# Local attention layers: norm products and half of a key projection placed between the halves of the products with values

## The chip, the cores and the metric

The kernel runs on one core of a Trainium2 chip. A core has five engines with instruction streams of their own: TensorE (PE; its weight loads are shown as PEld), VectorE (DVE), ScalarE (ACT), GpSimd (POOL) and SyncE (SP, which here issues the DMAs). They meet at semaphores. TensorE reads SBUF and writes PSUM. The metric is the device time of one execution in microseconds, and the median of several runs is compared.

## The reference

The program is two transformer blocks over an input of 4 sequences x 512 tokens x 128 features, float32. The first has causal attention with 16 heads and a mixture of experts, the second causal attention with 4 heads and, as its second half, a small network of six layers with local attention. The change touches only those six layers. Cut to what matters, one of them is:

```python
qkv = shift_tokens(x) @ Wqkv                 # 16 heads of 64
q = l2norm(q) * qs ;  k = l2norm(k) * ksc    # divided by the norm over the 64 features
q, k = rotary(q), rotary(k)
# windows of 32 tokens: each query window sees the window before it and its own
sim = einsum('bhwie,bhwje->bhwij', bq, bk2) * 8.0    # 32 x 64 for each window
attn = softmax(where(mask, -big, sim))
out = einsum('bhwij,bhwje->bhwie', attn, bv2)
x = out @ Wo + x
x = ffn(shift_tokens(x)) + x                 # layer norm, gated GELU, 128 -> 2 x 341 -> 128
```

## The kernel before, in words

The local layers hold the features on the partitions and 512 tokens of one sequence in the free dimension. The work is cut into *cells*: one cell is one layer, one sequence and a group of 4 heads, so there are 6 x 4 x 4 = 96. Four cells in a row share a sequence; after the fourth comes the feed-forward part of that sequence, `feed`, a generator cut in pieces that `place("N")`, `place("L")`, ..., `place("D")` put between the steps of later cells, one piece at a place of the right name.

The order of the instructions on each engine is the order in which the program emits them (`tc.manual_schedule()`); no planner moves anything. The loop over `n` works on several cells at once: it computes scores and attention of cell `n`, the last products with values of cell `n-1`, the norms and values of cell `n+2`, and the projections of cell `nx = n+3`. These are the steps that matter here, with their lines in the profile of before:

- `project(n, w)` (L831): queries (`w = 0`) or keys (`w = 1`), two products 128 x 128 by 128 x 512, the halves `h = 0, 1` of one PSUM tile `pq` of which there is a single buffer.
- `rotate` (L842, L843 on DVE, L844, L845 on POOL) reads `pq` into `qr` or `kr`; `square` (L850 on ACT) reads it too, into `sq`, and with that `pq` is free.
- `norms` (L860): eight products with 32 output rows each sum the squares into a PSUM tile `nb`; then DVE's maximum (L869), Ln and Exp on ACT with a table load each (L871, L873), and four DMAs by SP that spread the factors into `rb` (L879). `scale` (L887 on POOL) multiplies `kr` and `qr` by them.
- `values` (L898): four products into two PSUM tiles, copied by ACT (L905) and shifted by three DMAs.
- `scores(n, u)`, `u = 0, 1` (L921 masks, L928): 64 small products of 32 x 32 by 32 x 64, then DVE's maximum and subtraction (L937, L939). `exponential` (L948), `normalise` (L953 to L955), `turn` (L962 transposes on TensorE, L964 copy `pT` by ACT).
- `weigh(n, u)` (L977): 32 small products of 64 x 64 by 64 x 32 of `pT` with the values, into two PSUM tiles `po2` and `po2b`, copied out by ACT (L989). `po2b` shares its buffer with the transposes.
- `output` (L997) and `feed` (L1010 hidden products `phf`, L1015 gelu, L1025, L1033, L1061).

Each of these float32 products stands in the trace as two matmul records with two weight loads. The PSUM tiles `nb`, the values' two, the output's and all of feed's come from one pool of two buffers (`bank`).

TensorE's order in one turn of the loop is: `scores(n, 0)`, `weigh(n-1, 1)`, `norms(n+2)`, sometimes a piece of feed, `project(nx, 0)`, in every other cell `output`, `scores(n, 1)`, `values(n+2)`, sometimes a piece of feed, `turn(n, 0)`, `project(nx, 1)`, `weigh(n, 0)`, a piece of feed, `turn(n, 1)`. ScalarE's is: copies of `weigh(n-1, 1)`, `exponential(n, 0)`, Ln and Exp of the norms, `square(nx, 0)`, copies of values, `exponential(n, 1)`, `pT` of `turn(n, 0)`, copies of `weigh(n, 0)`, `pT` of `turn(n, 1)`, `square(nx, 1)`, and after that a piece of feed (in two cells of four one or two gelus with a table load).

Of the kernel before, what the change touches and what calls it, by code (L numbers as in the profile page):

```python
# [17 lines left out]
F32 = mybir.dt.float32  # L18
BF16 = mybir.dt.bfloat16
AF = mybir.ActivationFunctionType  # L20
ALU = mybir.AluOpType
# [3 lines left out]
B, S, D = 4, 512, 128  # L25
P = 128
# [20 lines left out]
def adaln_kernel(ctx: ExitStack, tc: tile.TileContext, a: dict):  # L47
# [4 lines left out]
    vec, pool_e = nc.vector, nc.gpsimd  # L52
# [192 lines left out]
    chain, rush, dense, norms = [], [], [], []  # L245
# [268 lines left out]
    def project(b):  # L514
        hT = zT[b]
        qk = io.tile([P, 2, 4, S], F32, name="qk0", bufs=3)
        v = io.tile([P, TB, H0 + 3, HD0 + 1], F32, name="v0")
        proj[b] = qk, v.rearrange("p t h d -> p t (h d)")
        for j in range(4):
            pp = ps_s.tile([P, 2, S], F32, name="pp", tag="s")  # L520
            for w in range(2):
                mm(pp[:, w, :], wqk[:, w, j, :], hT, start=True, stop=True)
            if j % 2 == 0:
                vec.tensor_scalar(
                    qk[:, 0, j, :], pp[:, 0, :], sb[:, 0, 1 + j : 2 + j], sb[:, 0, 0:1], ALU.add, ALU.mult
                )
                vec.tensor_scalar(qk[:, 1, j, :], pp[:, 1, :], sb[:, 1, 1 + j : 2 + j], None, ALU.add)
            else:
                act(qk[:, 0, j, :], pp[:, 0, :], AF.Identity, bias=sbq[:, j : j + 1], scale=sb[:, 0, 0:1])
                act(qk[:, 1, j, :], pp[:, 1, :], AF.Identity, bias=sb[:, 1, 1 + j : 2 + j])  # L530

            if j in (0, 3):
                js = slice(0, 1) if j == 0 else slice(1, 4)
                for w, row in ((0, HD0 + 1), (1, HD0)):
                    nc.sync.dma_start(qk[row::32, w, js, :], a["pos0"][w, :, js, :])
            if j in (0, 3):
                done.update(("project", b, x) for x in range(j + 1))
            yield
        pv = ps.tile([P, S], F32, name="pv0", tag="small")
        for t in range(TB):  # L540
            mm(pv[:, t * P : (t + 1) * P], hT[:, t * P : (t + 1) * P], wv, start=True, stop=True)


        pool_e.memset(v[:, :, H0:, :], 0.0)
        pool_e.memset(v[:, :, 0:H0, HD0 : HD0 + 1], 1.0)
        for t in range(TB):
            vec.tensor_tensor(
                v[:, t, 0:H0, 0:HD0],
                pv[:, t * P : (t + 1) * P].rearrange("p (h d) -> p h d", h=H0),
                bv.rearrange("p (h d) -> p h d", h=H0),  # L550
                ALU.add,
            )
        done.add(("values", b))
        yield
# [171 lines left out]
    while todo or late or ripe or pend:  # L726
        admit()
        if todo and (todo[0][1] or todo[0][0].start()):
            u, s = todo.pop(0)
# [37 lines left out]
    with ExitStack() as ph:  # L767
# [13 lines left out]
        def bank(name, shape=(P, S)):  # L781
            return ps_g.tile(list(shape), F32, name=name, tag="g")
# [9 lines left out]
        NC = len(cells)  # L792
# [29 lines left out]
            pool_e.tensor_scalar(t, t, g, None, ALU.mult)  # L822


        def project(n, w):
            l, b, j = cells[n]
            d = live.setdefault(n, {})
            pq = d["pq"] = ps_q.tile([P, 2, S], F32, name="pq")
            for h in range(2):
                c0 = w * INNER + (2 * j + h) * P  # L830
                mm(pq[:, h, :], layers[l][0][:, c0 : c0 + P], shifted[b], start=True, stop=True)  # L831

# [18 lines left out]

        def norms(n):

            d = live[n]
            nb = bank("nb", (P, S // 2))
            for h in range(2):
                for w in range(2):
                    for x in range(2):
                        c = 32 * (2 * w + x)
                        mm(  # L860
                            nb[c : c + 32, :],
                            nsel,
                            d["sq", w][:, h, x * (S // 2) : (x + 1) * (S // 2)],
                            start=(h == 0),
                            stop=(h == 1),
                            skip_group_check=True,
                        )
            rn = att.tile([P, S // 2], F32, name="rn")
            vec.tensor_scalar(rn, nb, 1e-24, None, ALU.max)  # L869
            place("N")  # L870
            act(rn, rn, AF.Ln, scale=65536.0)  # L871
            place("L")
            act(rn, rn, AF.Exp, scale=-0.5, bias=nsh_t)  # L873
            place("X")
            rb = d["rb"] = work.tile([P, 2, S], F32, name="rb", bufs=1)
            for w in range(2):
                for x in range(2):
                    c = 32 * (2 * w + x)
                    nc.sync.dma_start(  # L879
                        rb[:, w, x * (S // 2) : (x + 1) * (S // 2)],  # L880
                        rn[c : c + 32, :].unsqueeze(1).broadcast_to([32, 4, S // 2]),
                    )
# [80 lines left out]
            pT = live[n]["pT", u] = att.tile([P, 4, P], F32, name="pT2")  # L963
            nc.scalar.copy(pT, pt)  # L964

        def weigh(n, u):
            d = live[n]
            pT = d.pop(("pT", u))

            po = [ps_o.tile([P, 2, 4, WIN], F32, name="po2"), ps_t.tile([P, 2, 4, WIN], F32, name="po2b", tag="pt2")]  # L970
            for i in range(4):
                for x in range(4):
                    c = 64 * (x % 2)
                    for w in range(2):
                        r = slice(64 * w, 64 * w + 64)
                        c1 = 32 * ((x + w) % 4)
                        mm(  # L977
                            po[w][c : c + 64, x // 2, i, :],
                            d["v"][(w + i) % 2][r, 2 * u + i // 2, 64 * x : 64 * x + 64],
                            pT[r, i, c1 : c1 + 32],  # L980
                            start=True,
                            stop=True,
                        )
            if u == 0:
                d["o"] = cel.tile([P, 2, 2, S // 2], F32, name="oT2", bufs=3)
            o = d["o"][:, u].rearrange("p h (a w q) -> p (h a) w q", w=4, q=WIN)
            for w in range(2):
                y = po[w].rearrange("p h (a b) q -> p (h a) b q", b=2)
                nc.scalar.copy(o[:, :, 0::3, :] if w else o[:, :, 1:3, :], y)  # L989
# [93 lines left out]
        for n in range(-4, NC + 1):  # L1083
            nx = n + 3 if 0 <= n + 3 < NC else None
            here = 0 <= n < NC
            if here:
                scores(n, 0)
            if 0 <= n + 1 < NC:
                scale(n + 1)
            if n > 0:  # L1090
                weigh(n - 1, 1)
            if here:
                exponential(n, 0)
            if 0 <= n + 2 < NC:
                norms(n + 2)
            elif n + 2 >= NC:
                for name in "NLX":
                    place(name)
            place("C")
            if nx is not None:  # L1100
                l, b, j = cells[nx]
                if l + 1 < DEPTH:
                    if (b, j) == (2, 0):
                        layers[l + 1] = load_layer(l + 1)
                    if (b, j) == (2, 1):
                        load_rotations(l + 1)
                project(nx, 0)
            if here:
                normalise(n, 0)
            if nx is not None:  # L1110
                rotate(nx, 0)
            if n > 0 and cells[n - 1][2] % 2 == 1:
                output(n - 1)
            place("Z")
            if n + 4 < NC and cells[n + 4][2] == 0:
                b = cells[n + 4][1]
                shifted[b] = shift_in(b, xss[b % 2])
            if here:
                scores(n, 1)
            if nx is not None:  # L1120
                square(nx, 0)
            if 0 <= n + 2 < NC:
                values(n + 2)
            if here:
                exponential(n, 1)
            place("A")
            if here:
                turn(n, 0)
                normalise(n, 1)
            if nx is not None:  # L1130
                project(nx, 1)
                rotate(nx, 1)
            if here:
                weigh(n, 0)
            place("B")
            if here:
                turn(n, 1)
            if nx is not None:
                square(nx, 1)
                l, b, j = cells[nx]  # L1140
                for b1, j1, w, h in turns:
                    if (b1, j1) == (b, j) and l + 1 < DEPTH:
                        rotations(l + 1, w, h)
            place("D")
# [107 lines left out]
```

## Time and profile before

| | |
|---|---|
| three runs | 2582.3, 2593.25, 2601.71 us; median 2593.25 us |
| the profiled execution | 2575.9 us, span 2574.1 us, mean granted TensorE clock 0.955 |
| local layers | from 647 to 2569 us of the span, 96 cells |
| PE busy / weight loads | 2292.4 us (89%) / 1365.4 us (53%), 45916 instructions each |
| DVE, ACT, POOL busy | 1511.2 us (59%), 1402.9 us (55%), 1068.7 us (42%) |
| the chain that ended last | PE 73%, issue 9%, DVE 8%, ACT 8% |
| DMA queues | q1: data, 21.8% of 16 engines; q8: instructions, 359 packets, 5.88 MB |

How to read it: a row of the groups names line, engine, operation, tiles written and read, shapes and count, then the busy time and the mean length of one in ns, then the time the engine stood idle just before these instructions and what ended it. "issue" there means that nothing in the profile was waited for. The rows of the timeline begin with the start in us and the length. The matmuls overlap, so the distance between the starts of two records tells what one costs, not its length.

### The profile page before, as it was taken

What the parts mean: (1) busy time and instruction counts of PE and PEld (TensorE: products, weight loads), DVE (VectorE), ACT (ScalarE), POOL (GpSimd) and SP (SyncE); (2) the same over time, 40 slices, a digit from 0 to 9 for tenths busy, and PEclk for the clock granted to TensorE, in tenths of its full rate; (3) what the DMA queues carried; (4) which work ended last, traced back from release to release, by engine and by line L of the source; (5) the groups of instructions that cost most, each with busy time, mean ns of one, the idle gap of its engine ahead of it and who ended that gap; (6) DMA issues with size and microseconds to landing.
All of it is one profiled execution on the core that took longest, in us unless ns stands there. A gap on an engine that the chain in (4) does not pass through costs nothing.

```text
span 2574.1 us, 99974 instructions
## 1 busy us (share of the span) xinstructions
PE 2292.4 (89%) x45916; PEld 1365.4 (53%) x45916; DVE 1511.2 (59%) x2258; ACT 1402.9 (55%) x2211; POOL 1068.7 (42%) x692
## 2 busy tenths in 40 slices
PE   7899999877689999989999899998999899999997
PEld 3345454442355555556555555555555555556553
DVE  3354544343466666666666676665666667666763
ACT  1233336433456666566566566665665656666653
POOL 1000100110644664446545465544754546545540
PEclk9899999898888999989999999999999999999998
DMA  2100000000224222242222432234222333232220
GB/s 71 62 3 1 2 2 1 1 1 25 66 55 131 71 59 66 66 124 59 65 68 58 124 74 59 64 90 111 51 69 64 99 91 73 52 74 59 63 74 14
DMA packets 103408, 152.01 MB, mean 59 GB/s; under 512 B 16454, under 2 KB 78092, under 8 KB 101964
## 3 DMA queue, kind: packets, MB, share of 16 engines
q1 hardware_dynamic: 102988, 145.63, 21.8%
q8 instruction: 359, 5.88, 1.0%
q14 instruction: 61, 0.50, 0.1%
HBM read 34.27 MB, written 1.05 MB: 14 GB/s over the span
## 4 chain that ended last, share of the span: by engine, by line
PE 73%; issue 9%; DVE 8%; ACT 8%; DMA 1%; SPq 1%; POOL 1%; ACTq 0%; DVEq 0%; POOLq 0%
PE pq L831 12%; PE s L928 8%; PE py L997 6%; PE po L977 6%; PE phf L1010 5%; PE pv L898 5%; PE s L286 4%; PE nb L860 4%; PE pt L962 3%; PE pyf L1061 3%; PE ye L360 2%; PE po2b L977 2%; PE p L342 2%; DVE ur L843 1%; DVE qr L842 1%
## 5 line engine op out<-in xcount | busy, mean ns | idle before, releaser
L831 PE MATMUL pq<-xs,wqkv 128*128 128x512 f32 x768 | 395.5, 640 | 13.6 <-ACT sq L850 11.8
L844 POOL TENSOR_TENSOR kr<-kr,ur 128x512 f32<-128x512 f32 x96 | 122.1, 1272 | 540.1 <-DVE ur L843 512.6
L928 PE MATMUL s<-kr,qr 32*32 32x64 f32 x24576 | 296.9, 224 | 25.8 <-issue 25.6
L928 PEld LDWEIGHTS s<-kr,qr 32*32 32x32 f32 x24576 | 260.0, 103 | 71.8 <-issue 70.5
L850 ACT ACTIVATE sq<-pq 128x1024 f32<-128x1024 f32 x192 | 197.1, 1027 | 127.0 <-DVE ur L843 115.8
L937 DVE TENSOR_REDUCE nm<-s 128x8 f32<-128x512 f32 x192 | 132.2, 689 | 207.6 <-PE s L928 207.4
L844 POOL TENSOR_TENSOR qr<-qr,ur 128x512 f32<-128x512 f32 x96 | 122.8, 1279 | 309.4 <-DVE ur L843 276.1
L831 PEld LDWEIGHTS pq<-xs,wqkv 128*128 128x128 f32 x768 | 142.2, 204 | 172.9 <-issue 153.4
L887 POOL TENSOR_TENSOR qr<-qr,rb 128x1024 f32<-128x1024 f32 x96 | 233.3, 2430 | 0.0
L843 DVE TENSOR_TENSOR ur<-pq,tabs 128x1024 f32<-128x1024 f32 x192 | 232.9, 1213 | 0.0
L887 POOL TENSOR_TENSOR kr<-kr,rb 128x1024 f32<-128x1024 f32 x96 | 228.0, 2375 | 8.2 <-DMA rb<-rn 8.2
L989 ACT COPY oT<-po 128x256 f32<-128x256 f32 x192 | 71.4, 372 | 287.1 <-PE po2b L977 263.8
L964 ACT COPY pT<-pt 128x512 f32<-128x512 f32 x192 | 112.7, 587 | 193.5 <-PE pt L962 193.5
L404 ACT ACTIVATE p<-s 128x1024 f32<-128x1024 f32 (+3 forms) x160 | 104.0, 701 | 189.0 <-PE s L286 148.9
L173 POOL TENSOR_TENSOR ln_rs<-ln_rs,mhalf 128x4 f32<-128x4 f32 x16 | 16.8, 1049 | 436.9 <-DVE ln_rs L172 436.9
L953 DVE TENSOR_REDUCE sm<-p 128x8 f32<-128x512 f32 x192 | 130.6, 680 | 110.7 <-ACT p L948 110.5
L898 PE MATMUL pv<-wqkv,xs 128*128 128x256 f32 x768 | 191.2, 392 | 0.7 <-DVE qr L842 0.7
L977 PE MATMUL po<-pT,vo 64*64 64x32 f32 x3072 | 168.2, 224 | 19.7 <-issue 13.2
L977 PE MATMUL po2b<-pT,vo 64*64 64x32 f32 x3072 | 166.8, 222 | 19.3 <-issue 19.3
L977 PE MATMUL po<-pT,ve 64*64 64x32 f32 x3072 | 166.7, 222 | 19.0 <-issue 19.0
L977 PEld LDWEIGHTS po<-pT,vo 64*64 64x64 f32 x3072 | 129.1, 136 | 96.3 <-ACT pT L964 61.8
L977 PE MATMUL po2b<-pT,ve 64*64 64x32 f32 x3072 | 167.5, 224 | 11.0 <-issue 10.9
(198 smaller groups left out, 4954.6 us busy)
## 6 DMA issues: line engine op xcount, KB each, us to landing
rb<-rn SPq DMA_DIRECT2D x384, 128.0 KB
ve<-vo SPq DMA_DIRECT2D x96, 256.0 KB
tabs<-in_rope_dram SPq DMA_DIRECT2D x12, 1024.0 KB
ve<-vo SPq DMA_DIRECT2D x96, 128.0 KB
wqkv<-in_Wqkv_dram SPq DMA_DIRECT2D x6, 1536.0 KB
ve<-vo SPq DMA_DIRECT2D x96, 96.0 KB
wo<-in_Wo_dram SPq DMA_DIRECT2D x6, 512.0 KB
xs<-zT SPq DMA_DIRECT2D x24, 128.0 KB
```

Of the source, the lines that this page charges most:

```text
L831: mm(pq[:, h, :], layers[l][0][:, c0 : c0 + P], shifted[b], start=True, stop=True)
L843: vec.tensor_tensor(u, d["pq"], t[:, 2 * w + 1], ALU.mult)
L844: pool_e.tensor_tensor(r[:, 0, :], r[:, 0, :], u[:, 1, :], ALU.subtract)
L850: act(d["sq", w], d.pop("pq"), AF.Square)
L887: pool_e.tensor_tensor(t, t, d["rb"][:, w, :].unsqueeze(1).broadcast_to([P, 2, S]), ALU.mult)
L898: mm(pv[:, t, :], shifted[b][:, (y + t) * P : (y + t + 1) * P], layers[l][0][:, c0 : c0 + 4 * HDW], start=True, stop=True,)
L928: mm(s[c : c + 32, w, i, :], q[r, h, t0 : t0 + WIN], k[r, h, t0 : t0 + GK], start=False, stop=(h == 1), skip_group_check=True,)
L937: vec.reduce_max(nm, s, axis=AX.X)
L953: vec.reduce_sum(sm, p, axis=AX.X)
L977: mm(po[w][c : c + 64, x // 2, i, :], d["v"][(w + i) % 2][r, 2 * u + i // 2, 64 * x : 64 * x + 64], pT[r, i, c1 : c1 + 32], start=True, st ...
L997: mm(py, layers[l][1][:, 2 * j - 2 + y, :], o[:, :, y % 2, :], start=(y == 0), stop=(y == 3))
L1010: mm(t[0:m], w1[:, w * DI + r0 : w * DI + r0 + m], xn, start=True, stop=True)
```

## The change

`norms` is cut in two: the products stay in `norms`, and the maximum, Ln, Exp and DMAs become `factors`, at the place where all stood before. `weigh` gets a function to call between its second and third index `i`, that is after 16 of its 32 products. For `weigh(n-1, 1)` this function is `norms(n+2)`; for `weigh(n, 0)` it is the second half (`h = 1`) of `project(nx, 1)`, whose first half stands ahead of `weigh(n, 0)`. `rotate(nx, 1)` is now emitted after `weigh(n, 0)`; on the engines that it uses, DVE and POOL, nothing of weigh stands, so the order there is the same. The orders of ACT, DVE, POOL and SP are as before; TensorE's is not. Computation, tiles and buffers are the same.

```diff
-        def project(n, w):
+        def project(n, w, halves=(0, 1)):
             l, b, j = cells[n]
             d = live.setdefault(n, {})
-            pq = d["pq"] = ps_q.tile([P, 2, S], F32, name="pq")
-            for h in range(2):
+            if 0 in halves:
+                d["pq"] = ps_q.tile([P, 2, S], F32, name="pq")
+            pq = d["pq"]
+            for h in halves:
                 c0 = w * INNER + (2 * j + h) * P
...
         def norms(n):
 
+            if not 0 <= n < NC:
+                return
             d = live[n]
-            nb = bank("nb", (P, S // 2))
+            nb = d["nb"] = bank("nb", (P, S // 2))
...
+
+        def factors(n):
+
+            d = live[n]
             rn = att.tile([P, S // 2], F32, name="rn")
-            vec.tensor_scalar(rn, nb, 1e-24, None, ALU.max)
+            vec.tensor_scalar(rn, d.pop("nb"), 1e-24, None, ALU.max)
...
-        def weigh(n, u):
+        def weigh(n, u, middle):
...
             for i in range(4):
+                if i == 2:
+                    middle()
                 for x in range(4):
...
             if n > 0:
-                weigh(n - 1, 1)
+                weigh(n - 1, 1, lambda: norms(n + 2))
+            else:
+                norms(n + 2)
             if here:
                 exponential(n, 0)
             if 0 <= n + 2 < NC:
-                norms(n + 2)
+                factors(n + 2)
...
+            def half(h):
+                if nx is not None:
+                    project(nx, 1, (h,))
+
+            half(0)
+            if here:
+                weigh(n, 0, lambda: half(1))
+            else:
+                half(1)
             if nx is not None:
-                project(nx, 1)
                 rotate(nx, 1)
-            if here:
-                weigh(n, 0)
```

## The prediction

> **What bounds the kernel now.** I read the page first, then TensorE's timeline in the local layers, then the list of waits, then a table of short stretches for the clock.
>
> The page says who is busy and how many instructions TensorE has to be fed:
>
> ```profile
> PE 2292.4 (89%) x45916; PEld 1365.4 (53%) x45916; DVE 1511.2 (59%) x2258; ACT 1402.9 (55%) x2211; POOL 1068.7 (42%) x692
> ...
> q8 instruction: 359, 5.88, 1.0%
> ...
> L928 PE MATMUL s<-kr,qr 32*32 32x64 f32 x24576 | 296.9, 224 | 25.8 <-issue 25.6
> ...
> L977 PE MATMUL po<-pT,vo 64*64 64x32 f32 x3072 | 168.2, 224 | 19.7 <-issue 13.2
> ```
>
> TensorE is busy 89% of the span; in the local layers (647 to 2569 us, 96 cells, 20.0 us each) one block follows on the other. So every TensorE moment there counts, and an edit on another engine counts only where TensorE waits for it. Second, 45916 matmuls and as many weight loads came in 359 instruction packets: 91832 / 359 = 256 instructions a packet. Third, both small-tile groups lose idle time to "issue", which is no other engine. The timeline shows what that is, here in the middle of one weigh block:
>
> ```profile
> 1508.79 0.22 PE L977 MATMUL po<-pT,ve 64*64 64x32 f32 x1
> 1510.31 0.19 PE L977 MATMUL po2b<-pT,vo 64*64 64x32 f32 x1 [1.31 <-issue]
> ```
>
> Counted over the matmul records, 41 gaps above 0.25 us stand inside weigh blocks (71.7 us) and 28 inside scores blocks (31.8 us), practically all at a record whose number leaves 193 or 194 on division by 256. Work resumes about 2.3 to 2.7 us after an instruction packet started, and packets that follow each other fastest start 3.3 to 3.5 us apart. So I read: 256 instructions that run in less than about 3.4 us make TensorE wait for the next 256. A scores block is 256 instructions in 1.41 us and a weigh block 128 in 0.93, and `scores(n, 0)` and `weigh(n-1, 1)` stand back to back. What such a gap can cost on top is in the table of stretches (busy times, then granted clock, DMA share, GB/s):
>
> ```profile
> 1034.30:1037.70 3.40, 1.66 (x125) 1.46 (x108) 1.38 (x2) 3.37 (x5) 3.40 (x3) 1.00 0.03 7
> 1037.70:1041.10 3.40, 3.31 (x19) 1.39 (x19) 1.11 (x2) 3.06 (x5) 3.34 (x2) 0.50 0.02 5
> ```
>
> After a stretch with TensorE half idle the next 3.4 us run at half clock. Between 646 and 2560 us the half clock holds for 126 us, some 63 us of work lost.
>
> **The part that saves.** At the first join the eight norm products stand between the halves of weigh. If the boundary falls into the second half (64 instructions a cell, so 96 x 64 / 256 = 24 boundaries), the last 256 instructions now took 0.70 (128 of scores) + 0.13 (leaving scores) + 0.23 (half of the second weigh half) + 0.60 (first half and its exit) + 1.1 (norms) = 2.75 us where they took 0.88 + 0.13 + 0.70 = 1.7. The wait falls from 1.7 to 0.65: 24 x 1.05 = **-26 us**. A boundary in scores, in the first half or in the norms themselves (2.2 us there after, 2.3 before) waits as long as now. At the second join there is nothing to save: `weigh(n, 0)` follows values, transposes and a projection, over 4 us with few instructions.
>
> **More changes of tile shape.** The sum needs what it costs TensorE to go from one tile shape to another. Three pairs of rows of its timeline, each the last record of a block and the first of the next:
>
> ```profile
> 1512.88 1.02 PE L831 MATMUL pq<-xs,wqkv 128*128 128x512 f32 x2
> 1513.73 0.59 PE L997 MATMUL py<-oT,wo 128*128 128x512 f32 x1
> ...
> 1522.44 0.59 PE L831 MATMUL pq<-xs,wqkv 128*128 128x512 f32 x1
> 1522.96 0.24 PE L977 MATMUL po<-pT,vo 64*64 64x32 f32 x1
> ...
> 1523.88 0.22 PE L977 MATMUL po2b<-pT,vo 64*64 64x32 f32 x1
> 1524.03 1.09 PE L1010 MATMUL phf<-l_xc,w 128*85 128x512 f32 x2
> ```
>
> Same shape: two pq records take 0.85 to py, 0.43 each. From pq to weigh: 0.52, so 0.09 for the change. From weigh: 0.15 to the next shape, where weigh's own records follow at 0.0147, so 0.135. The first pq after another shape takes 0.53 to the second, 0.10 more. First join: weigh is left once more, 0.135. Second join: pq left once more 0.09, weigh left once more 0.135, pq entered once more 0.10: 0.33. Together 0.46 a cell, x 96 = **+44 us**. The step from norms into weigh is in no row of the trace; norms into pq takes 0.31 against 0.21 for four norms records and I take the same. Ends 30 and 60. This is also where a rule speaks against the change: the Trainium skill, TensorEngine Tiling, Key Properties, says that changing the tiling mode (not the tile) drains TensorE. It gives no figure; a full drain by the records' lengths would be 0.22 - 0.015 at each of two exits from weigh and 0.59 - 0.43 at one from pq, 0.57 a cell, 55 us. The rows say 44, and I take them.
>
> **Less cover for the transposes' copy.** `weigh(n, 0)` needs pT, which ScalarE copies last of its row of work:
>
> ```profile
> 1521.40 0.64 ACT L948 ACTIVATE p<-p 128x512 f32<-128x512 f32 x1
> 1521.93 0.58 ACT L964 COPY pT<-pt 128x512 f32<-128x512 f32 x1
> ```
>
> pT stands at 1522.51, weigh starts at 1522.96: 0.45 spare, because a whole key projection lies in front. With half of it (2 records of 0.43) weigh is reached 0.86 earlier. In four cells in a row the spare time is 0.05, 0.45, 1.03, 0.46 (weigh at 1503.30, 1522.96, 1542.24, 1563.13), and 0.05 of it is the semaphore. New waits: 0.86, 0.46, 0, 0.45; mean 0.44, x 96 = **+42 us**. Nothing wins that back: the other half of the projection comes later in full. Ends 30 and 55. Behind the waiting weigh stand the second half of pq and all else on TensorE; rotate, which needs both halves, was 0.1 to 1.8 us late for other reasons and slips by about as much as TensorE.
>
> **The norms come earlier, the weigh copies later.** The list of waits has both places:
>
> ```profile
> PE phf L1010 <- ACT vo L905: 29.3, 22, 1.8
> ...
> PE nb L860 <- ACT ge L1015: 16.2, 20, 1.0
> ```
>
> The norms' PSUM bank is one that a gelu frees, in two cells of four. Norms are reached 0.46 earlier, so the 20 waits grow by that, 9 us, and the 28 such cells without a wait by a little: **+12** (0 to 22). Half of weigh is now queued behind the wait. Its copies by ScalarE, and the exponential behind them, come later by the norms and the change of shape, 1.1 us, in every cell. In most this is lost in slack: the copies of values wait 0.3 to 1.5 us for TensorE in the plain cells, or normalise's multiply waits out GpSimd's product with the scales anyway (started at 1571.61 it took 2.31 us, and 0.69 where GpSimd is idle). It isn't in the cell with the third gelu: there weigh ended at 1529.20 and the copies ran at 1529.85; now the norms wait until 1530.0, weigh ends near 1531.7, the table load that began at 1530.49 begins near 1532.4, 1.9 later. Exponential, normalise, rotate, square, the copies of values follow in line, and phf waits for those. TensorE itself is 0.6 later, so the 1.4 us wait grows by 1.3 (0 to 1.7): 22 x 1.3 = **+29 us**. The norms' own way (maximum, Ln, Exp, four DMAs by SP) still comes behind that exponential, and its result is needed a cell later.
>
> **Half clock.** Of the gaps between 1.5 and 2.1 us 7 in 36 were followed by half clock, of those above 2.1 us 7 in 12; the cost is 1.7 us or more each. 24 gaps shrink (5 fewer episodes), 22 grow to near 2.7 us (up to 12 more): **+10**, between -15 and +25. The Trainium skill, TensorE: Matmul & The Clock Gate, asks for no idle gap over about 3 us. By that neither kind of gap would count and the term would be 0; the rows above show half clock after 1.8 us, so I keep it.
>
> **Sum.** -26 + 44 + 42 + 12 + 29 + 10 = +111 us. The profiled execution took 2575.9 us (span 2574.1, 1.8 around it), giving 2687; the median of the runs shown is 2593.25, giving 2704. I say **2695**, between the two.
>
> **Rivals.** (1) *Faster by better fetching.* If the spacing took away all of weigh's issue gaps (72 us) and half of the half-clock loss (30), and pT proved hidden, -102 + 44 = -58: about 2520 to 2535. It decides only from 86 us of gain on, the shape changes plus pT, more than all weigh gaps together. For it: the gaps stand where the norms go. Against: scores are left whole, so boundaries in the first half of weigh and in the norms (96 of 160 instructions) wait as before, and those in the second half still 0.65. (2) *No change*: changing shape is hidden under the pT wait and the 1.3 us of phf don't come: 42 - 26 - 10 = +6, about 2590. Against: the shape rows are the same in every cell. (3) *Much slower*: the 1.1 us later exponential goes through to pT in every cell, since ScalarE's work is one line: 96 x 1.1 = 106 more, about 2800. Against: the slack in the plain cells. (4) *Milder*: half of the costs, +40 to +60, about 2640.
>
> **Numbers.** Forecast 0.66, milder 0.10, much slower 0.10, no change 0.08, faster 0.06. The unknown costs span about +55 to +175; the range 2625 to 2765 leaves out (1), (2) and most of (3). A measurement of this kernel can tell about 1% from no change: slower 0.86, same 0.08, faster 0.06.
>
> **What would show it.** Right: waits of weigh for pT grow from some 60 to over 100 us; phf's for the copies of values from 29 to near 60; norms' for gelu grow; issue gaps in weigh fall from 72 to about 45, in scores they stay; a TensorE step of 0.15 stands between weigh and norms twice a cell. Wrong: pT waits unchanged, or issue gaps down by more than 60, or the half clock down by more than half.

## The result, and the profile after

The changed kernel takes 2713.52 us (median of 4 runs, 2708.16 to 2716.03) against 2587.78 us of the kernel before: ratio 1.0479, 95% interval 1.0424 to 1.0534, 126 us slower. The forecast was 2695 in a range of 2625 to 2765. The profiled execution took 2716.03 us with a span of 2714.1.

From the page of the changed kernel, the rows that answer to those shown of before, and one that was small before:

```profile
PE 2366.7 (87%) x45916; PEld 1386.5 (51%) x45916; DVE 1510.0 (56%) x2258; ACT 1401.2 (52%) x2211; POOL 1064.4 (39%) x692
...
L936 PE MATMUL s<-kr,qr 32*32 32x64 f32 x24576 | 290.6, 224 | 9.9 <-issue 9.6
...
L1022 PE MATMUL phf<-l_xc,w 128*128 128x512 f32 (+1 forms) x288 | 170.3, 722 | 63.5 <-ACT vo L913 59.5
...
L989 PE MATMUL po<-pT,vo 64*64 64x32 f32 x3072 | 176.6, 227 | 54.1 <-ACT pT L972 45.1
```

The same 45916 matmuls, but TensorE is shown busy 74 us longer (the granted clock is 0.945 after 0.955) and idle 66 us longer. In the last row pT has taken the place of "issue" as the main reason for idle time ahead of weigh, and the idle time ahead of scores has fallen from 25.8 to 9.9 us, which the prediction did not have. The list of waits has the three places that grew, and the two that shrank:

```profile
PE phf L1022 <- ACT vo L913: 59.5, 22, 3.3
...
PE po L989 <- ACT pT L972: 45.1, 75, 2.6
...
PE nb L864 <- ACT ge L1027: 40.9, 34, 1.4
...
PE po L989 <- issue: 26.7, 18, 5.0
...
PE s L936 <- issue: 9.6, 10, 1.9
```

Before, phf waited 29.3 us and the norms 16.2, in the rows shown ahead; the other three were

```profile
PE po L977 <- issue: 32.2, 19, 4.3
...
PE s L928 <- issue: 25.6, 26, 3.3
...
PE po L977 <- ACT pT L964: 6.3, 4, 2.1
```

Each row gives the total in us, how many times, and the longest.

For the balance I use the local layers alone, from the first projection's record to TensorE's last, since no edit touches what stands ahead of them and that part varies with the clock (647 to 668 us in the profiles). "Busy" is TensorE's busy time there and "half" the time at half clock, busy or not. "Gaps" are the issue gaps over 0.25 us inside blocks of weigh and scores, from the start of one record to the start of the next. The last four columns are waits. All are in us, each row from one profiled execution, which lies up to 17 us from its kernel's median (before: 12 under it), so a few us between two rows carry no weight.

| kernel | local | busy | half | gaps weigh | gaps scores | weigh for pT | norms for gelu | phf for values | pq for square |
|---|---|---|---|---|---|---|---|---|---|
| before | 1922 | 1742 | 138 | 72 | 32 | 6 | 16 | 29 | 12 |
| changed | 2056 | 1810 | 186 | 52 | 13 | 45 | 41 | 60 | 16 |
| second join only | 1977 | 1773 | 124 | 72 | 14 | 42 | 18 | 32 | 10 |
| first join only | 1984 | 1761 | 155 | 52 | 34 | 6 | 38 | 59 | 13 |
| product again, inside | 2019 | 1845 | 124 | 81 | 10 | 5 | 20 | 33 | 10 |
| product again, ahead | 1999 | 1814 | 121 | 85 | 11 | 5 | 18 | 37 | 13 |
| changed, exponential first | 1943 | 1760 | 80 | 52 | 10 | 41 | 40 | 14 | 8 |
| changed, turn first | 1987 | 1779 | 124 | 46 | 14 | 12 | 45 | 50 | 20 |
| before, exponential first | 1905 | 1736 | 121 | 72 | 25 | 5 | 16 | 23 | 13 |
| queries between | 1913 | 1750 | 145 | 16 | 34 | 5 | 0 | 63 | 36 |
| changed, both moves | 1889 | 1749 | 66 | 39 | 18 | 9 | 43 | 6 | 9 |
| before, both moves | 1915 | 1742 | 148 | 83 | 25 | 2 | 19 | 18 | 12 |
| before, exponential and values first | 1867 | 1721 | 93 | 74 | 22 | 5 | 17 | 0 | 12 |
| queries between, values first | 1841 | 1722 | 73 | 15 | 38 | 5 | 0 | 9 | 42 |

The expectations below use an earlier count of the half clock that left out stretches at both ends of the local layers (113 us before, 174 changed, 133 with the queries between).

The changed kernel's 134 us in the local layers are then 66 us of idle time (local less busy: 181 to 247 us) and 68 us of busy time. The idle time is phf +30, pT +39, gelu +25, square +4, issue -32 (as gaps from start to start -39: weigh -20, scores -19). Of the busy time some 24 us are half clock, if half of the 48 us more at half speed is lost. The other 44 us no wait explains, and the steps between tile shapes were put at 44. These steps stand in the trace. At full clock and without a wait, the changed kernel takes in the median 0.149 us from weigh to pq (150 times), 0.522 from pq to weigh (102), 0.309 from norms to weigh (85) and 0.533 from the first pq record after weigh to the next (149), where pq after the transposes takes 0.432.

### The profile page after: what moved, and what is told of

It reads as the page before. It is cut to its first block, busy times and chain, and to the rows that moved or that the text cites. A ratio compares the mean times of both kernels' runs of the same rounds, so it can differ in the third digit from the quotient of the medians.

```text
span 2714.1 us, 99997 instructions
## 1 busy us (share of the span) xinstructions
PE 2366.7 (87%) x45916; PEld 1386.5 (51%) x45916; DVE 1510.0 (56%) x2258; ACT 1401.2 (52%) x2211; POOL 1064.4 (39%) x692
## 3 DMA queue, kind: packets, MB, share of 16 engines
HBM read 34.27 MB, written 1.05 MB: 13 GB/s over the span
## 4 chain that ended last, share of the span: by engine, by line
PE 67%; ACT 17%; DVE 8%; issue 7%; DMA 1%; POOL 1%; ACTq 0%; SPq 0%; DVEq 0%; POOLq 0%
PE pq L833 9%; PE po L989 7%; PE py L1009 6%; PE phf L1022 6%; PE s L936 6%; PE s L286 4%; PE nb L864 4%; PE pv L906 4%; PE pyf L1073 2%; ACT vo L913 2%; ACT p L956 2%; PE ye L360 2%; PE pt L970 2%; ACT pT L972 2%; ACT sq L852 2%
## 5 line engine op out<-in xcount | busy, mean ns | idle before, releaser
L833 PE MATMUL pq<-xs,wqkv 128*128 128x512 f32 x768 | 422.2, 655 | 19.3 <-ACT sq L852 16.0
L936 PE MATMUL s<-kr,qr 32*32 32x64 f32 x24576 | 290.6, 224 | 9.9 <-issue 9.6
L1022 PE MATMUL phf<-l_xc,w 128*128 128x512 f32 (+1 forms) x288 | 170.3, 722 | 63.5 <-ACT vo L913 59.5
L989 PE MATMUL po<-pT,vo 64*64 64x32 f32 x3072 | 176.6, 227 | 54.1 <-ACT pT L972 45.1
L833 PEld LDWEIGHTS pq<-xs,wqkv 128*128 128x128 f32 x768 | 133.2, 201 | 103.0 <-issue 71.1
```

Of the source, the lines that this page charges most:

```text
L936: mm(s[c : c + 32, w, i, :], q[r, h, t0 : t0 + WIN], k[r, h, t0 : t0 + GK], start=False, stop=(h == 1), skip_group_check=True,)
L989: mm(po[w][c : c + 64, x // 2, i, :], d["v"][(w + i) % 2][r, 2 * u + i // 2, 64 * x : 64 * x + 64], pT[r, i, c1 : c1 + 32], start=True, st ...
L1022: mm(t[0:m], w1[:, w * DI + r0 : w * DI + r0 + m], xn, start=True, stop=True)
```

## The experiments

**Each join by itself.** `e1_second_join` keeps the cut of the key projection and puts the norms back behind weigh; `e2_first_join` keeps the norms in the middle and puts the key projection back ahead of weigh.

```diff
 # second join only
-                weigh(n - 1, 1, lambda: norms(n + 2))
+                weigh(n - 1, 1, lambda: None)
...
+                norms(n + 2)
                 factors(n + 2)
 # first join only
             half(0)
+            half(1)
             if here:
-                weigh(n, 0, lambda: half(1))
+                weigh(n, 0, lambda: None)
```

> Only the second join of the change: half of the key projection ahead of weigh(n, 0), half in its middle; the norms stand whole behind weigh(n-1, 1) as before. Theory (shape changes and lost cover for pT): 0.33 us x 96 = 32 us for the extra shape changes and about 40 us of new waits of weigh for pT, so +70 us, ratio 1.027, with issue gaps in weigh (72 us), phf's waits (29 us) and norms' waits for gelu (16 us) as before. Rival (the late copies and the long gaps of the first join are all of the loss): under +20 us.

> Only the first join: the norm products in the middle of weigh(n-1, 1); the key projection whole ahead of weigh(n, 0) as before. Theory: 0.135 x 96 = 13 us of shape changes, +25 us of waits for gelu, +30 us of phf's waits, +20 to 30 us of half clock behind phf's long gaps, less 20 to 39 us of issue gaps: about +55 us, ratio 1.021, so that both joins add up to the whole change (+126). pT waits as before (6 us). Rival (shape changes and pT are all): about +13 us less the issue gaps, so zero or faster.

Second join: 2638.32 us, ratio 1.0169 (1.0145 to 1.0193). First join: 2639.68 us, ratio 1.0186 (1.0149 to 1.0224). Expected were 1.027 and 1.021: by these ratios the second join costs 26 us less than expected, the first 6. Their waits, second join and then first:

```profile
PE po L989 <- ACT pT L972: 41.6, 74, 2.1
...
PE phf L1022 <- ACT vo L913: 32.2, 22, 3.9
```

```profile
PE phf L1022 <- ACT vo L913: 59.4, 22, 3.4
...
PE nb L864 <- ACT ge L1027: 37.9, 30, 1.5
...
PE po L989 <- ACT pT L972: 6.4, 4, 2.6
```

The waits part cleanly: pT belongs to the second join, phf and gelu to the first. pT's 42 us stand there without the late copies of the first join, so those don't reach pT. The second join alone takes the scores gaps from 32 to 14 us, most of what it cost less than expected, and the first join alone the weigh gaps from 72 to 52. The times add up to 90 us, the whole change to 126. Half clock accounts for some 22 us of the difference: alone the two joins change it by -14 and +17 us, together by +48, and half of that is lost.

**The price of a change of tile shape.** `e3_again_inside` and `e4_again_ahead` are the kernel before with one half of the key projection computed twice, the second time in the middle of weigh, or directly ahead of it.

```diff
             if nx is not None:
                 project(nx, 1)
-                rotate(nx, 1)
+                again(nx)                          # e4: mm of half h = 1 once more
             if here:
-                weigh(n, 0)
+                weigh(n, 0, lambda: again(nx))     # e3, in place of the line above
+            if nx is not None:
+                rotate(nx, 1)
```

> The kernel before, with the second half of the key projection computed a second time in the middle of weigh(n, 0), into the same place; the whole projection still stands ahead of weigh, so pT has its full cover, and rotate comes behind weigh. Theory: the product itself 0.86 us x 96 = 82 us and the shape changes 0.33 x 96 = 32 us: +114 us. To be read against the run that follows, which has the same product without a new shape change. Rival (shape changes cost nothing where the queue is full): +82 us.

> The same second computation of half a key projection, but ahead of weigh(n, 0), directly behind the projection. No new shape change. Theory: 82 us for the product, less the 6 us of remaining waits for pT that it covers: +76 us, so some 35 us less than with the product in the middle. Rival: no difference between the two beyond 6 us.

Inside: 2683.34 us, ratio 1.0335 (1.0306 to 1.0365). Ahead: 2672.57 us, ratio 1.0298 (1.0262 to 1.0335). The medians differ by 11 us where 32 was expected, and the intervals overlap, so the times alone don't show the price. The two profiled executions do, as far as one of each can: inside, TensorE is idle 11 us less (174 against 185) and busy 31 us more, with half clock level (124 and 121 us). Some 29 us are left for the cut, and they are no wait. The other part of the sum holds too: ahead, with 8 us of half clock set off, the product itself costs some 81 us of busy time, where 82 was expected.

**The exponential ahead of the copies.** In `e5_after_exp_first` only one call of the changed kernel moves, and with it one instruction a cell on ScalarE.

```diff
+            if here:
+                exponential(n, 0)
             if n > 0:
                 weigh(n - 1, 1, lambda: norms(n + 2))
             else:
                 norms(n + 2)
-            if here:
-                exponential(n, 0)
```

> The changed kernel with exponential(n, 0) emitted ahead of weigh(n-1, 1), so that on ScalarE it no longer stands behind the copies of weigh. Nothing else moves. Theory (phf's growth from 29 to 59 us is the exponential queued behind the later copies, and half clock follows from these gaps): phf's waits fall below 30 us, half clock in the local layers from 174 to near 115 us, 60 us faster than the changed kernel: ratio about 1.024. Waits for gelu and for pT stay (41 and 45 us). Rival (phf waits because the norms themselves are late, through gelu): phf's waits stay near 59 us and the time near 1.048.

2608.94 us, ratio 1.011 (1.0066 to 1.0154): of the 126 us lost, some 100 come back. What happened shows in ScalarE's timeline in the cell of the third gelu, first in the changed kernel:

```profile
1002.62 0.68 ACT L1027 ACTIVATE ge<-phf,prm 85x512 f32<-85x512 f32 x1
1005.08 0.37 ACT L1001 COPY oT<-po 128x256 f32<-128x256 f32 x1 [1.77 <-PE po2b L989]
...
1007.03 0.63 ACT L956 ACTIVATE p<-p 128x512 f32<-128x512 f32 x1
...
1012.62 1.07 ACT L913 COPY vo<-pv 128x512 f32<-128x512 f32 x2
```

and then with the exponential first:

```profile
984.80 0.68 ACT L1027 ACTIVATE ge<-phf,prm 85x512 f32<-85x512 f32 x1
...
986.79 0.63 ACT L956 ACTIVATE p<-p 128x512 f32<-128x512 f32 x1
987.33 0.35 ACT L1001 COPY oT<-po 128x256 f32<-128x256 f32 x1
...
992.59 1.07 ACT L913 COPY vo<-pv 128x512 f32<-128x512 f32 x2
```

After the gelu ScalarE stood idle for 1.77 us until the second half of weigh was done, and the exponential, which needs nothing of weigh, stood behind that: it began 4.4 us after the gelu had begun, now 2.0. The copies of values follow 10.0 and 7.8 us after the gelu. phf's waits fall to 14 us, and the half clock from 186 to 80 us:

```profile
PE phf L1022 <- ACT vo L913: 13.5, 21, 1.0
```

The norms still wait 40 us for gelu, so it was not their lateness that phf paid for. Here is the clock at one such wait in the changed kernel (busy times of PE, PEld, DVE, ACT and POOL, then granted clock, DMA share and GB/s):

```profile
1009.80:1013.20 3.40, 0.69 (x4) 0.26 (x2) 3.10 (x4) 2.90 (x5) 1.44 (x2) 1.00 0.15 25
1013.20:1016.60 3.40, 3.34 (x4) 1.41 (x5) 0.75 (x1) 1.02 (x3) 1.04 (x1) 0.50 0.90 238
```

TensorE waits 2.77 us for phf's bank, and the 3.4 us behind it run at 0.50. Of 27 gaps over 2.6 us in the changed kernel, 17 have half clock beginning in them or within 1 us of their end.

**The transposes' copy ahead of the other exponential.** In `e9_after_turn_first` the changed kernel emits `turn(n, 0)` earlier.

```diff
             if here:
+                turn(n, 0)
                 exponential(n, 1)
             place("A")
             if here:
-                turn(n, 0)
                 normalise(n, 1)
```

> The changed kernel with turn(n, 0) emitted ahead of exponential(n, 1), so that ScalarE copies pT before that exponential. The second join stays cut as in the change. Theory (weigh(n, 0) waits for pT because half a projection is too little cover for ScalarE's line): pT comes 0.6 us earlier, its waits fall from 45 us to some 20 us, 20 to 25 us faster than the changed kernel: ratio about 1.039. Shape changes are untouched. Rival (the wait is the array's change of shape under another name): pT waits and time stay.

2650.89 us, ratio 1.025 (1.0198 to 1.0302), a gain of some 60 us in place of 25. The waits for pT fall as the theory says and further:

```profile
PE phf L1022 <- ACT vo L913: 49.5, 22, 3.0
...
PE po L989 <- ACT pT L972: 11.9, 28, 2.2
```

33 us come from pT and 10 from phf; half clock goes from 186 to 124 us, some 31 more, which I had not counted. It accounts for all of the busy time saved (1810 to 1779 us), so the shape changes are untouched. So the wait is ScalarE's order, not the array's change of shape.

**The same cure on the kernel before, and another spacing.** `e6_before_exp_first` moves the exponential in the kernel before (the same edit as above). `e8_queries_between` has that too, and moves a whole block of large products into the dense stretch:

```diff
             if here:
                 scores(n, 0)
             if 0 <= n + 1 < NC:
                 scale(n + 1)
+            if nx is not None:
+                project(nx, 0)       # with the loads of the next layer, as they stood
             if here:
                 exponential(n, 0)
             if n > 0:
                 weigh(n - 1, 1)
...
-                project(nx, 0)
```

> The kernel before with exponential(n, 0) emitted ahead of weigh(n-1, 1); TensorE's order is as before. Theory: the exponential comes up to 0.65 us earlier in the cells with a gelu, phf's waits fall from 29 us to about 16 us and some half clock goes with them: 15 to 25 us faster than before, ratio 0.992. Rival (the line of ScalarE has slack there): ratio 1.00.

> The kernel before with exponential(n, 0) ahead of weigh(n-1, 1), and the query projection of cell nx moved from behind the norms to between scores(n, 0) and weigh(n-1, 1): 8 instructions of 1.7 us in the middle of the dense stretch. Theory (TensorE stalls when 256 instructions run in under 3.4 us): weigh's issue gaps fall from 72 us to under 15 us, gaps in scores stay near 30; waits for gelu vanish; one more shape change costs 18 us; the norms come 2 us later, which may bring some 30 us of waits of the key projection for square. Sum about -35 us, ratio 0.986. Rival (the gaps come from something in weigh itself, not from the rate of instructions): gaps stay near 70 us, ratio 1.015.

With the exponential first: 2566.95 us, ratio 0.9928 (0.9907 to 0.9949), as expected in size; phf's waits fall to 23 us, not to 16. Queries between: 2568.25 us, ratio 0.9947 (0.9911 to 0.9983), where 0.986 was expected: no faster than with the exponential first alone. Its waits:

```profile
PE phf L1010 <- ACT vo L905: 63.4, 22, 4.8
...
PE pq L831 <- ACT sq L850: 36.0, 25, 3.7
...
PE po L977 <- issue: 7.7, 4, 2.7
```

Weigh's issue gaps fall from 72 to 16 us with weigh itself untouched: what counts here is how long 256 instructions take. The gain is spent on two waits, square as expected and phf, which I had not expected to double.

**Both moves on ScalarE, with the change and without.** `e10_after_exp_turn_first` is the changed kernel with both moves, `e13_before_exp_turn_first` the kernel before with both, as its control.

> The changed kernel with both moves on ScalarE's line: exponential(n, 0) ahead of weigh(n-1, 1) and turn(n, 0) ahead of exponential(n, 1). What is left of the change then are its shape changes (44 us) and the waits of the norms for gelu (25 us more than before), against 39 us of issue gaps saved. Theory: pT's waits near 12 us, phf's near 14 us, local layers near 1910 us: level with the kernel before within 1%, ratio 0.995 to 1.005, and about 10 us slower than the kernel before with the exponential first. Rival (the two moves get in each other's way on ScalarE or VectorE): ratio above 1.01.

> The kernel before with the same two moves on ScalarE's line as in the run with both on the changed kernel: exponential(n, 0) ahead of weigh(n-1, 1), turn(n, 0) ahead of exponential(n, 1). It is the control for that run: the two differ in the change alone. Theory (once ScalarE's line no longer carries the change's cost, it is shape changes and gelu waits against issue gaps, -39 - 7 for the gaps and +44 + 27 for the rest, half clock aside): this one is 10 to 25 us faster than the changed kernel with both moves, local layers near 1875 us, ratio near 0.98. Rival (the spacing pays, with half clock saved): this one is slower than the changed kernel with both moves, ratio 0.993 as with the exponential first alone.

With the change: 2550.71 us, ratio 0.9885 (0.9821 to 0.995). Without: 2566.41 us, ratio 0.9922 (0.9895 to 0.9949). My expectation failed: the control is not 10 to 25 us faster. The intervals overlap, so that the change is a gain here is not shown; but its loss of 4.8% is gone. Among the control's waits:

```profile
PE po2b L977 <- issue: 39.4, 26, 3.7
...
PE po L977 <- issue: 33.3, 20, 5.4
...
PE nb L860 <- ACT ge L1015: 18.6, 22, 1.5
```

It has 108 us of gaps and 148 us of half clock where the kernel with the change has 56 and 66. Against that stand 24 us more of gelu waits in the kernel with the change, and its shape changes. I had left half clock aside. The control has 82 us more of it, some 41 us lost, and its local layers took 1915 us where I expected 1875. The busy times of this pair, with half clock set off, differ by 48 us, those of the two kernels with the exponential first by 44: the price of the shape changes once more.

**A faster version.** The idea is that phf waits for the copies of values because these stand behind `square(nx, 0)`, and so behind rotate. `e11_before_exp_values_first` is the kernel before with the exponential first, and with `values(n + 2)` ahead of `square(nx, 0)` in the cells where hidden products of feed follow the values (there the list `gated` is filled); `e12_queries_between_values_first` has the queries between as well.

```diff
-            if nx is not None:
+            if nx is not None and not gated:
                 square(nx, 0)
             if 0 <= n + 2 < NC:
                 values(n + 2)
+            if nx is not None and gated:
+                square(nx, 0)
```

> The kernel before with exponential(n, 0) ahead of weigh(n-1, 1) and, in the cells where gate's hidden products follow the values, the copies of values ahead of square(nx, 0). Theory (phf waits because the copies of values stand behind square, which stands behind rotate): phf's waits fall from 23 us to under 8, half clock goes down with them: 20 us faster than with the exponential first alone, ratio 0.985. Rival (the copies wait for TensorE's values anyway): as with the exponential first alone, 0.993.

> The kernel with the query projection between scores(n, 0) and weigh(n-1, 1) and the exponential first, and the copies of values ahead of square(nx, 0) in the cells of the gate. Theory: issue gaps in weigh stay near 16 us, phf's waits fall from 63 us to under 15, half clock from 133 us to near 80; waits of the key projection for square stay near 38 us. 60 to 70 us faster than without the last move: ratio about 0.970. Rival (what phf loses square gives back, as the key projection waits longer): ratio 0.985 or above.

2531.72 us, ratio 0.9808 (0.9742 to 0.9874), and 2493.3 us, ratio 0.9657 (0.9603 to 0.9711): 92 us faster than the kernel before. In the first, phf no longer waits at all. In the second, phf's waits fall from 63 to 9 us, and those for square, expected near 38, grow only from 36 to 42, so the gain is not spent there; the issue gaps in weigh stay at 15 us:

```profile
PE pq L831 <- ACT sq L850: 42.1, 34, 3.7
...
PE phf L1010 <- ACT vo L905: 9.1, 14, 0.8
```

## Why the prediction was right, and where it was not

The sign, the size (126 us against 102 to 111) and the main reason hold: TensorE is the bound, and the change gives it more waits and shape changes than it saves. That the sum came so close is in part luck: a saving in scores that was not foreseen sets off most of what gelu and half clock cost more. By its steps:

- **Weigh's second half, -26 us** (24 x 1.05 is 25). Held: 23 gaps with 44.9 us before, 13 with 13.1 us after. The first half went the other way, from 18 gaps with 26.8 us to 21 with 38.7, since the order decides where in a block each 256th instruction falls; net -20.
- **"At the second join there is nothing to save."** Wrong by 18 us. Half of a projection now stands inside the 256 instructions that reach from weigh over the transposes into the next scores, and a boundary in scores waits less. With the second join alone, the boundaries at the same records do so: at record 101 of one block 1.04 us in place of 2.24. I had looked at boundaries in weigh alone.
- **Shape changes, +44 us.** The sum held, 44 us without a wait to explain them, and so did the steps one by one, each within 0.01 us. The one that no row of before showed, norms into weigh, is 0.31 us as assumed. By joins the balance is less sharp: 11 us for the first (13 expected), and for the second (32) 38 by the single join and 29 by the pair of runs. A full drain as the prediction estimated it, 55 us, is not seen.
- **pT, +42 us.** 39 measured, and one move on ScalarE takes 33 of them away.
- **Gelu, +12 us.** 25: the term that was mis-sized by half. The waits went from 20 to 34 and their mean from 0.8 to 1.2 us. I had given the 28 cells without a wait "a little"; half of them now wait.
- **phf, +29 us.** 30 measured, and the late exponential as its cause is shown.
- **Half clock, +10 us.** Some 24, the other mis-sized term. I had counted episodes of one stretch of 3.4 us, and 13 of the 34 in the changed kernel lasted two (6 of 27 before). The 126 us that I gave for before took stretches by their start; by time it is 138 in the local layers. The Trainium skill (TensorE: Matmul & The Clock Gate, Why this matters for your kernels) sets the limit at about 3 us, and the traces don't agree: in the changed kernel half clock begins in, or within 1 us behind, 8 of the 12 phf gaps of 2.8 us and 2 of the 5 of 3.3 us. In the kernel before it follows gaps from 1.4 us up, though not each of them.
- **Rivals.** Faster by better fetching: weigh's gaps fell by 20 and not by 72, so it did not decide. With ScalarE's line mended, gaps and half clock together outweigh the price in the two profiled executions; the times don't show it. Much slower: the late exponential doesn't reach pT (42 us without it, 45 with it).

What stays open: whether the change gains with both moves, and why some gaps of one length are followed by half clock and others not.

## What to carry to other kernels

When work is put into the middle of a block, look at what waits for the block's end on every in-order engine: here a copy that nobody needed soon stood ahead of an exponential that a chain of four steps needed, and moving one call won back some 100 of 126 us. A stretch of many small matmuls had a second limit here, the rate at which its instructions arrive. Large products in between took weigh's gaps from 72 to 16 us, and the length of the last 256 instructions told where a gap would be long. Count what an idle gap costs afterwards in clock, not only its own length.

## What the runs showed of the hardware

- TensorE stalls in the middle of a block of independent small matmuls, at fixed places 256 instructions apart, when these ran in under about 3.4 us: 104 us in 69 gaps before, all at the same two places in the count of 256. The Trainium skill, Runtime: NRT & Kernel Launch, Instruction fetch mechanics, has the refill in blocks of 256 instructions but calls its cost mostly hidden; it isn't here.
- Half clock after a gap was worth as much as the gap: in the changed kernel 186 us in the local layers, at most 93 us of work. One moved instruction for each cell took 46 us of phf's waits away and 106 of the 186 us with them, at most 53 us of work.
- Changing the tile shape and back inside a block of weigh cost about 0.13 us for the norms in its middle, which had another shape on both sides before too, and 0.33 us for a full-array product, without any wait to be seen: some 44 us for 96 cells.
